# A selective scan on one core: diagonal matrices of B by way of DRAM scratch, and the next product ahead of the gate

## The chip, the core and the metric

The kernel runs on one core of one Trainium2 chip. A core has a matrix engine (PE; its weight loads are shown as PEld), a vector engine (DVE), a scalar engine (ACT), a general engine (POOL), a sync engine (SP) that here issues most of the DMAs, and 16 DMA engines. The engines run their own instruction streams and wait for each other by semaphores. The metric is the device time of one execution in microseconds, lower is better; it is the median of several runs.

## The reference

Two residual layers on x of shape 8 x 128 x 128 x 128. The first (Fourier and window attention over channels, with depthwise convolutions) is not touched by the change. The second is a Mamba block over the 16384 pixels of each image, and the change is in its scan:

```python
xz = u @ W_in
xs, z = jnp.split(xz, 2, axis=-1)
xt = conv_general_dilated(xs.T, conv_w, ...) + conv_b      # 4 taps, causal
xc = jax.nn.silu(xt)
dt, Bm, Cm = jnp.split(xc @ W_xproj, [DT_RANK, DT_RANK + D_STATE], axis=-1)
delta = jax.nn.softplus(dt @ W_dt + b_dt)
def step(hs, inp):
    d_t, B_t, C_t, u_t = inp
    dA = jnp.exp(d_t[:, :, None] * A)
    h_new = dA * hs + (d_t * u_t)[:, :, None] * B_t[:, None, :]
    y_t = jnp.einsum('bdn,bn->bd', h_new, C_t)
    return (h_new, y_t)
y = ys + xc * D_param
out = (y * silu(z)) @ W_out
```

There are 256 channels d and 16 states n, so 4096 recurrences per image, each 16384 long, in float32.

## The kernel before

The scan part cuts each image into 32 chunks of 512 pixels (`T`), 256 chunks in all. A chunk has 16 steps (`ST`). A step works on a tile of 128 partitions (4 states by 32 channels) by 512 pixels, twice (`j` = 0 and 1): so 32 scans a chunk. `where(n)` turns the running step number n into chunk, half of the channels `h` (steps 0 to 7 and 8 to 15), pair of states `mp` (0 in steps 0 to 3 and 8 to 11, else 1) and block `k`.

In step n these stand in the engines' queues:

- `product(n+1)`: on PE, 32 small matmuls that form delta*u*B for the next step in PSUM (`hb`, two buffers). The weights are `duT`, the transposed delta*u of 64 pixels; the moving operand is `bd`, 64 x 64 diagonal matrices that hold B of two states, so that a matmul multiplies each pixel by its own B. The trace counts each float32 matmul twice, so 64 per product.
- `decay(n+3)`: on ACT, two exponentials `dA`.
- `scan(n)`: on DVE, two scans `hs` over `dA` and `hb`.
- `keep_state(n-1)`: on ACT, the last column of `hs`, for the next chunk.
- `weigh(n)`: on POOL, `hc` = `hs` times C (`crep`, C repeated over partitions by DMAs).

The rest of a chunk's work is spread over the steps by a hand-written table, `beside`: a step, a chunk relative to the current one, and a function. `first` is a second table of two entries, `gate` at step 3 and `step_sizes_act` at step 7, both for the next chunk; its entries stand ahead of decay and product. Work on PE beside the products: four taps of `conv` for each half, `gate` (e_z), `xproj` (e_x), `step_sizes` (e_dt), `turn_b` (e_bt, the transposed B), `turn` (e_t), `add` (y, sums over states), `project` (e_o). On DVE beside the scans: `skip` (yt), `residual` (acc), and the diagonals. On POOL beside `weigh`: `drive` (du) and `gated` (yt).

The diagonals of B before the change: `turn_b` at step 7 transposes B on PE into PSUM, `keep_b` at step 8 copies it to `bt` with DVE. `diagonals` multiplies the constant `same` (two identity matrices of 64) with B, 1 of 8 blocks (128 x 512) at a time; DVE makes six blocks a chunk. `more_diagonals` makes the other two as 16 activations of 128 x 64 on ACT. `bd` has two buffers, one for each `mp`.

`InOrder` (lines 169 to 187) records the compute instructions of each engine so that they run in the order written; therefore nearly all instructions carry line 180 in the profile, and are told apart by their tiles. DMAs on SP are not bound by it: they stand in the order in which a scheduler put them, and SP issues them strictly one after the other. A DMA on SP also waits until the eighth DMA before it has landed.

DMAs of a chunk, all on SP: `xin` (line 1063, the input two chunks ahead, 256 KB), `cd` (line 1131, C to DRAM), `crep` (line 1140, 4 x 128 KB for `mp` 0 after `cd`, and 4 more for `mp` 1), `dld` (line 1155, delta to DRAM, 512 KB) and `dlrep` (line 1161, delta repeated over partitions, 4 x 256 KB for each half). `crep` has three buffers and `dlrep` two, so that the second half of each waits until POOL and ACT are done with an older one. Every eighth chunk a band of the image is loaded for the residual (`acc`, line 1069, 2 MB in runs of 128 bytes), and a finished band is stored by ACT's queue (2 MB, runs of 128 bytes).

Of the kernel before, what the change touches and what calls it, by code (L numbers as in the profile page):

```python
# [111 lines left out]
def _layout(a):  # L112

    a = {n: np.asarray(v) for n, v in a.items()}
    o = {"x": np.ascontiguousarray(a["x"]).reshape(B, C, HW)}
    o["consts"], o["bconsts"], o["ker"] = _constants()
    p = "L0_conv_"
    f, s = a[p + "projf_w"].reshape(C, 2 * C), a[p + "projs_w"].reshape(C, 2 * C)

    rows = np.arange(C).reshape(2, 4, 16).transpose(1, 0, 2).reshape(-1)  # L120

    j, h = np.arange(8)[:, None], np.arange(NH)[None, :]
    frows = np.concatenate([(HD * h + j).reshape(-1), (HD * h + 15 - j).reshape(-1)])
    ws = [a[p + n + "1_w"].reshape(C, C) for n in "qkv"] + [f[:, frows], f[:, C:], s[:, rows], s[:, C:]]
    o["wpack"] = np.concatenate([w.T for w in ws] + [a[p + "w1"].reshape(NK, C).T], 1)
    tf = np.repeat(a[p + "temp_f"].reshape(NH), HD)
    ts = np.repeat(a[p + "temp_s"].reshape(NH), HD)[rows]
    o["cvec"] = np.stack([a[p + n + "1_b"] for n in "qkv"] + [tf, ts], 1)
    o["bn"] = np.concatenate([a[p + n] for n in ("b1", "bn_gamma", "bn_beta", "bn_mean", "bn_var")])[None]
    w2 = np.zeros((13, NK + 1, 13, C), np.float32)  # L130
    for u in range(13):
        w2[u, :NK, u] = a[p + "w2"].reshape(C, NK).T
        w2[u, NK, u] = a[p + "b2"]

    w2 = w2.reshape(13, NK + 1, 13, C // 8, 2, 4).transpose(0, 1, 4, 3, 5, 2)
    o["w2blk"] = w2.reshape(13 * (NK + 1), 13 * C)


    taps = np.zeros((4, NG, 2, 8, 8, 2, 4, 4), np.float32)
    for n, c in enumerate("qkvc"):  # L140
        for y in range(4):
            for x in range(4):
                taps[n, :, :, y + 1 : y + 4, x + 1 : x + 4, 0, y, x] = a[p + c + "3_w"]
                taps[n, :, :, y : y + 5, x : x + 5, 1, y, x] = a[p + c + "5_w"]
    taps = taps.reshape(4, NG // 4, 4, 2, 2, 4, 2, 4, 32)
    o["taps"] = taps.transpose(2, 3, 5, 7, 1, 0, 4, 6, 8).reshape(128, -1)
    p = "L1_conv_"
    o["win"] = a[p + "W_in"]
    o["cw"] = a[p + "conv_w"].T.reshape(1, 4 * DI)

    xp = a[p + "W_xproj"].reshape(2, 128, DR + 2 * DS).transpose(1, 0, 2)
    wx = np.zeros((128, 2, 4, 32), np.float32)
    wx[:, :, :2, :DR] = xp[:, :, None, :DR]
    wx[:, :, 2, :] = xp[:, :, DR:]
    o["wx"] = wx.reshape(128, 256)
    o["wdt"] = np.zeros((128, 128), np.float32)
    for h in range(2):
        o["wdt"][32 * h : 32 * h + DR] = a[p + "W_dt"][:, h * 128 : (h + 1) * 128]
    o["same64"] = np.tile(np.eye(64, dtype=np.float32), (2, 1))
    o["gath"] = np.tile(np.eye(32, dtype=np.float32), (4, 1))  # L160
    o["wout"] = a[p + "W_out"].reshape(2, 128, C).transpose(1, 0, 2).reshape(128, -1)
    halves = [a[p + n].reshape(2, 128).T for n in ("conv_b", "b_dt", "D_param")]
    o["dvec"] = np.concatenate(halves, 1)

    o["alog"] = a[p + "A_log"].reshape(DI // 32, 32, 4, 4).transpose(2, 1, 3, 0).reshape(128, -1)
    return {n: np.ascontiguousarray(v) for n, v in o.items()}
# [24 lines left out]
def tile_kernel(ctx: ExitStack, tc: tile.TileContext, I: dict, out: bass.AP):  # L191
# [830 lines left out]
    NQ, NM, NR, NBK = 4, 4, 32, DI // 32  # L1022
    ND, NTB = 64, T // 128
    QR = 32
    with tc.tile_pool(name="e_c", bufs=1) as cp, tc.tile_pool(name="e_w", bufs=2) as wk, tc.tile_pool(
        name="e_h", bufs=4
    ) as hp, tc.tile_pool(name="e_d", bufs=3, space=DRAM) as dp, tc.tile_pool(
        name="e_b", bufs=2, space=PSUM
# [4 lines left out]
            return t  # L1033

        gath = fixed("gath", [128, NR], I["gath"])
        same = fixed("same", [128, ND], I["same64"])
        unit = fixed("unit", [128, 128], I["consts"][:, 0:128])
        win = fixed("win", [128, 2 * DI], I["win"])
        wx = fixed("wx", [128, 2, 128], I["wx"])
        wdt = fixed("wdt", [128, 128], I["wdt"])  # L1040
        wout = fixed("wout", [128, 2, C], I["wout"])
# [3 lines left out]
        nc.scalar.activation(A, A, AF.Exp)  # L1045
        nc.vector.tensor_scalar(A, A, -1.0, None, ALU.mult)

        wf = cp.tile([128, 4, DI], F32, name="wf")
        nc.sync.dma_start(wf.rearrange("p a d -> p (a d)"), I["cw"].partition_broadcast(128))
        for k in range(4):  # L1050
            nc.vector.tensor_tensor(wf[:, k, :], wf[:, k, :], win[:, 0:DI], ALU.mult)
        state = cp.tile([128, NM, NBK], F32, name="state")
        ch = {}
        total = B * NCH
        RT = T // W
# [3 lines left out]

        def load(i):  # L1060
            b, k = divmod(i, NCH)
            xin = wk.tile([128, T], F32, name="xin")
            nc.sync.dma_start(xin, X1[b, :, k * T : (k + 1) * T])
            ch[i] = {"xin": xin}

# [45 lines left out]
        def gate(i):  # L1111
            c = ch[i]
            c["sz"] = wk.tile([128, 2, T], F32, name="sz", bufs=3)
            for h in range(2):
                ps = bank("e_z", h)
                pe.matmul(ps, lhsT=win[:, DI + h * 128 : DI + (h + 1) * 128], rhs=c["u"][:, 3:], start=True, stop=True)
                act.activation(c["sz"][:, h, :], ps, AF.Silu)

        def xproj(i):
# [29 lines left out]
        def step_sizes_act(i):  # L1149
# [5 lines left out]
            nc.sync.dma_start(d.rearrange("h p t -> p h t"), c["dl"])  # L1155
            for h in range(2):
                if h:
                    repeat_c(i, 1)
                t = c["dlr", h] = wk.tile([128, 4, T], F32, name="dlrep")
                for q in range(NQ):  # L1160
                    nc.sync.dma_start(t[q * NR : (q + 1) * NR], d[h].rearrange("(k r) t -> r k t", r=NR))
# [29 lines left out]
                pe.transpose(c["bp"][:, 32 * j : 32 * j + 32], c["dbl"][rs, j * 128 : (j + 1) * 128], unit[rs, rs])  # L1191

        def keep_b(i):
            c = ch[i]
            c["bt"] = wk.tile([128, NTB, DS], F32, name="bt")
            dve.tensor_copy(c["bt"], c["bp"][:, : NTB * 32].rearrange("p (j n) -> p j n", n=32)[:, :, :DS])

        def diagonals(i, mp, j):


            c = ch[i]
            if (mp, j) in ((0, 0), (1, 0)):
                c["bd", mp] = wk.tile([128, NTB, NQ, ND, 2], F32, name="bd")
            to = [128, NQ, ND, 2]
            b = c["bp"][:, 32 * j : 32 * j + DS].rearrange("p (q m) -> p q m", m=NM)[:, :, 2 * mp : 2 * mp + 2]
            dve.tensor_tensor(
                c["bd", mp][:, j], same.unsqueeze(1).unsqueeze(3).to_broadcast(to), b.unsqueeze(2).to_broadcast(to), ALU.mult
            )

        def more_diagonals(i, which):  # L1210

            c = ch[i]
            for n in which:
                j, q, m = 2 + n // 8, n // 2 % 4, n % 2
                at = NM * q + 2 + m
                act.activation(c["bd", 1][:, j, q, :, m], same, AF.Identity, scale=c["bt"][:, j, at : at + 1])


        ST = 16
# [11 lines left out]
        def decay(n):  # L1231
            i, h, mp, k = where(n)
            for j in range(2):
                dA = hp.tile([128, T], F32, name="dA", bufs=10)
                kk = 4 * h + k
                act.activation(dA, ch[i]["dlr", h][:, k, :], AF.Exp, scale=A[:, 2 * mp + j, kk : kk + 1])
                dAs[n, j] = dA
# [69 lines left out]
        def residual(i):  # L1307
# [10 lines left out]

        beside = [
            (0, 1, lambda i: conv(i, 1, 2)),  # L1320
            (0, 0, lambda i: diagonals(i, 1, 1)),
            (0, 0, lambda i: more_diagonals(i, range(6, 11))),
            (1, 1, lambda i: conv(i, 1, 3)),
            (1, 0, lambda i: more_diagonals(i, range(11, 16))),
            (2, 1, conv_act),
            (2, -1, lambda i: add(i, 3, 0, 1)),
            (3, -1, lambda i: skip(i, 1)),
# [3 lines left out]
            (5, 0, lambda i: add(i, 0, 0)),  # L1331
            (6, 0, lambda i: add(i, 0, 1)),
            (6, 1, step_sizes),
            (7, 1, turn_b),
            (8, -1, project),
            (8, 1, lambda i: drive(i, 0)),
            (8, 1, keep_b),
            (8, 2, norm),
            (9, -1, residual),
            (9, 1, lambda i: drive(i, 1)),  # L1340
            (9, 2, lambda i: conv(i, 0, 0)),
            (10, 0, lambda i: add(i, 1, 0, 1)),
            (11, 0, lambda i: skip(i, 0)),
            (11, 1, lambda i: diagonals(i, 0, 0)),
            (11, 1, lambda i: turn(i, 0)),
            (11, 2, lambda i: conv(i, 0, 1)),
            (12, 0, lambda i: gated(i, 0)),
            (12, 1, lambda i: turn_act(i, 0)),
            (12, 1, lambda i: diagonals(i, 0, 1)),
            (12, 2, lambda i: conv(i, 0, 2)),  # L1350
            (13, 1, lambda i: diagonals(i, 0, 2)),
            (13, 1, lambda i: turn(i, 1)),
            (13, 2, lambda i: conv(i, 0, 3)),
            (14, 1, lambda i: turn_act(i, 1)),
            (14, 1, lambda i: diagonals(i, 0, 3)),
            (14, 0, lambda i: add(i, 2, 0, 1)),
            (15, 1, lambda i: diagonals(i, 1, 0)),
            (15, 1, lambda i: more_diagonals(i, range(6))),
            (15, 2, lambda i: conv(i, 1, 0, 1)),
        ]  # L1360
        first = [
# [4 lines left out]
        for n in range(-2 * ST, (total + 1) * ST):  # L1366
# [5 lines left out]
                    rows_of(i // NCH, i % NCH * RT)  # L1372
            if there((n - 1) // ST):
                keep_state(n - 1)
            for step, rel, f in first:
                if step == s and there(i + rel):
                    f(i + rel)
            if there((n + LEAD) // ST):
                decay(n + LEAD)
            if there((n + 1) // ST):  # L1380
                product(n + 1)
            if there(i):
                scan(n)
            for step, rel, f in beside:
# [23 lines left out]
```

## Time and profile before

| | |
|---|---|
| median of 3 runs | 18748.7 us (18740.43 to 18783.58) |
| profiled execution, first to last instruction | 18790.5 us |
| first scan to last | 6647 to 18763 us |
| chunk of the scan part, mean | 47.3 us |
| busy share of the whole span: PE, DVE, ACT, POOL | 88%, 76%, 64%, 70% |
| granted PE clock in the scan part | 0.99 of full speed |
| DMA engines busy in the scan part, mean | 0.45 |

The profile is of one execution. Busy time is the union of an engine's instructions; the idle time before an instruction is put down to what ended it: another engine, a DMA, or "issue" when the profile shows nothing that the engine waited for. Steps are numbered 0 to 15 within a chunk; a step is between 2.4 us (two scans) and 4.7 us long. A window's table gives busy time per engine, so that a single chunk can be set beside the mean.

### The profile page before, as it was taken

The page shows a single profiled execution, that of the slowest core. Times are in us where ns is not written, and L with a number is a line of the kernel's source. Part 1 is how long each engine was busy: PE and PEld are TensorE (multiplying, and loading weights), DVE is VectorE, ACT ScalarE, POOL GpSimd, SP SyncE. Part 2 cuts the span into 40 slices and gives each one's busy share as a digit, 9 for nine tenths or more (in the row PEclk, how much of TensorE's full clock was granted, in tenths as well). Part 3 has the DMA queues.
Part 4 walks back from the last instruction along what each step waited for, and adds up shares of the span by engine and source line. Part 5 has one row for each costly group of instructions (what it writes and reads, how often), then busy time and mean ns, then how long its engine had stood idle before and what let it go on. Part 6 is the DMA issues. An engine that isn't in the chain of part 4 may idle for free. (4 is left out here: it accounts for less than half of the span.)

```text
span 18790.5 us, 791009 instructions
## 1 busy us (share of the span) xinstructions
PE 16559.7 (88%) x353336; PEld 9548.0 (51%) x353336; DVE 14247.0 (76%) x15987; ACT 12026.1 (64%) x26077; POOL 13091.3 (70%) x7572
## 2 busy tenths in 40 slices
PE   7789988888888888999899889998999999998898
PEld 5566665555555544444444444444444444444444
DVE  6545543333444489999999999999999999999998
ACT  4443333344323377777777777777777777777777
POOL 3333334443222278899899888998898888888898
PEclk8899998889999999999999999999999999999999
DMA  9963347777777645444544454445444444444443
GB/s 377 370 220 94 93 125 226 231 236 214 201 207 208 195 98 104 97 97 97 106 97 97 97 102 97 96 97 102 97 97 97 102 101 96 95 98 101 94 97 86
DMA packets 2434567, 2601.35 MB, mean 138 GB/s; under 512 B 1221965, under 2 KB 1624013, under 8 KB 2396866
## 3 DMA queue, kind: packets, MB, share of 16 engines
q1 hardware_dynamic: 1730850, 2206.28, 44.1%
q10 hardware_dynamic: 679840, 277.32, 7.2%
q8 instruction: 2783, 45.60, 1.1%
q0 software_dynamic: 20480, 67.13, 1.1%
q14 instruction: 614, 5.03, 0.1%
HBM read 1715.23 MB, written 834.93 MB: 136 GB/s over the span
## 5 line engine op out<-in xcount | busy, mean ns | idle before, releaser
L180 POOL TENSOR_TENSOR hc<-hs,crep 128x1024 f32<-128x1024 f32 x4096 | 9646.3, 2372 | 1262.6 <-DVE hs L180 813.8
L180 DVE TENSOR_TENSOR_SCAN hs<-dA,state,hb 128x512 f32<-128x512 f32 x7936 | 9578.7, 1262 | 817.5 <-PE hb L180 744.1
L180 PEld LDWEIGHTS hb<-bd,duT 64*32 64x32 f32 x262144 | 3747.2, 106 | 3720.4 <-issue 2751.1
L180 PE MATMUL hb<-bd,duT 64*32 64x128 f32 x262144 | 4925.6, 275 | 708.2 <-issue 504.2
L180 ACT ACTIVATE dA<-dlrep,A 128x512 f32<-128x512 f32 x8192 | 5443.4, 713 | 7.9 <-ACT state L180 1.7
L180 PE MATMUL e_xc<-u,wf 128*128 128x512 f32 x4096 | 2236.0, 639 | 408.2 <-ACT u L180 361.5
L180 PE MATMUL y<-hc,gath 128*32 128x512 f32 x16384 | 2078.5, 609 | 36.8 <-issue 34.5
L180 ACT COPY state<-hs 128x2 f32<-128x2 f32 x4096 | 776.9, 190 | 1892.2 <-DVE hs L180 1874.1
L180 ACT ACT_TABLE_LOAD x1057 | 1356.1, 1283 | 338.9 <-PE e_dt L180 292.0
L180 PE MATMUL c_mm<-src,taps 32*32 32x512 f32 x32768 | 1219.9, 630 | 207.9 <-issue 175.4
L180 DVE COPY vst<-c_mm 128x512 f32<-128x512 f32 x1024 | 684.8, 689 | 741.9 <-PE c_mm L180 637.3
L180 PEld LDWEIGHTS e_xc<-u,wf 128*128 128x128 f32 x4096 | 646.5, 192 | 826.4 <-ACT u L180 430.8
L180 ACT ACTIVATE bd<-same,bt 128x64 f32<-128x64 f32 x4096 | 1054.2, 339 | 5.3 <-PE hb L180 5.1
L180 POOL TENSOR_SCALAR qm<-vst,cst 128x512 f32<-128x512 f32 x256 | 503.8, 2062 | 779.1 <-DVE vst L180 745.7
L180 PEld LDWEIGHTS c_mm<-src,taps 32*32 32x32 f32 x32768 | 680.5, 105 | 706.8 <-issue 518.3
L180 ACT ACTIVATE junk<-vst 128x256 f32<-128x256 f32 x1024 | 416.6, 410 | 942.5 <-DVE vst L180 941.3
L180 DVE TENSOR_TENSOR bd<-same,e_bt 128x512 f32<-128x512 f32 x1536 | 1019.4, 664 | 0.0
L180 PE MATMUL a_mm<-xt,wp 128*128 128x256 f32 x3072 | 763.2, 410 | 261.9 <-ACT pk L180 182.2
L180 POOL TENSOR_TENSOR eo<-eo,et 128x1008 f32<-128x1008 f32 x128 | 298.5, 2332 | 969.1 <-DVE et L180 960.6
L180 POOL DMA_DIRECT2D X<-d_x x256 | 138.4, 541 | 1072.2 <-DVE d_x L180 864.3
L180 DVE TENSOR_TENSOR d_x<-d_p,d_x 128x512 f32<-128x512 f32 x256 | 274.9, 1074 | 783.6 <-DMA d_x<-in_x 505.7
L180 PEld LDWEIGHTS a_mm<-xt,wp 128*128 128x128 f32 x3072 | 621.1, 206 | 419.5 <-ACT pk L180 195.5
(179 smaller groups left out, 19982.9 us busy)
## 6 DMA issues: line engine op xcount, KB each, us to landing
dlrep<-dld SPq DMA_DIRECT2D x2048, 256.0 KB
crep<-cd SPq DMA_DIRECT2D x2048, 128.0 KB
dld<-dl SPq DMA_DIRECT2D x256, 512.0 KB
src<-Pq SPq DMA_DIRECT2D x128, 544.5 KB
src<-Pv SPq DMA_DIRECT2D x128, 544.5 KB
src<-Pk SPq DMA_DIRECT2D x128, 544.5 KB
src<-Px SPq DMA_DIRECT2D x128, 544.5 KB
xt<-in_x SPq DMA_DIRECT2D x64, 1024.0 KB
```

Source lines behind the costliest of these rows:

```text
L180: made = method(*args, **kwargs)
```

## The change

It has these parts.

- `diagonals`, `more_diagonals` and `same` go. Four DRAM scratch tensors `diag` (128 rows of 2048 floats, 1 MB each; two per `mp`, used by alternate chunks) are filled with zeros once. `keep_b`, now an ACT copy, writes B of each chunk onto their diagonals by four DMAs of 64 x 16 runs of two floats. `load_b` loads a whole matrix back, 1 MB, as `bd`, which has three buffers now. `load_b` for `mp` 0 stands inside `step_sizes_act` behind the loads of `dlrep` for the first half, for `mp` 1 at step 8.
- `turn_b` goes from step 7 to 5, `keep_b` from 8 to 6, and `norm` (the input of the chunk after next, on ACT) from 8 to 6.
- In each step `product(n+1)` stands ahead of the table `first` and of decay. On PE that changes step 3 alone, where `gate` is in `first`.
- To make room: `win` keeps only the half that `gate` reads (the other is used once, for `wf`), `xin` has one buffer instead of two, `dA` nine instead of ten.

In the scheduled program SP's order for a chunk becomes: `cd`, `xin`, one write of `diag`, four `crep`, three writes of `diag`, `dld`, `load_b` for `mp` 0, four `dlrep`, four `crep`, four `dlrep`, `load_b` for `mp` 1. `load_b` for `mp` 0 waits for both writes to its tensor.

```diff
+    cp = ctx.enter_context(tc.tile_pool(name="e_c", bufs=1))
+    wf = cp.tile([128, 4, DI], F32, name="wf")
+    nc.sync.dma_start(wf.rearrange("p a d -> p (a d)"), I["cw"].partition_broadcast(128))
+    DROW = NTB * NQ * ND * 2
+    diag = {(n, mp): dram.tile([128, DROW], F32, name=f"diag{n}{mp}") for n in range(2) for mp in range(2)}
+    with tc.tile_pool(name="e_0", bufs=1) as zp:
+        win_x = zp.tile([128, DI], F32, name="win_x")
+        nc.sync.dma_start(win_x, I["win"][:, 0:DI])
+        for k in range(4):
+            nc.vector.tensor_tensor(wf[:, k, :], wf[:, k, :], win_x, ALU.mult)
+        zero = zp.tile([128, DROW], F32, name="zero")
+        nc.gpsimd.memset(zero, 0.0)
+        for d in diag.values():
+            nc.sync.dma_start(d, zero)
...
-            xin = wk.tile([128, T], F32, name="xin")
+            xin = wk.tile([128, T], F32, name="xin", bufs=1)
...
             for h in range(2):
                 if h:
+                    load_b(i, 0)
                     repeat_c(i, 1)
...
         def keep_b(i):
             c = ch[i]
-            c["bt"] = wk.tile([128, NTB, DS], F32, name="bt")
-            dve.tensor_copy(c["bt"], c["bp"][:, : NTB * 32].rearrange("p (j n) -> p j n", n=32)[:, :, :DS])
-
-        def diagonals(i, mp, j):
...
-        def more_diagonals(i, which):
...
+            bt = wk.tile([128, NTB, DS], F32, name="bt")
+            act.copy(bt, c.pop("bp")[:, : NTB * 32].rearrange("p (j n) -> p j n", n=32)[:, :, :DS])
+            for mp in range(2):
+                d = diag[i % 2, mp]
+                for x in range(2):
+                    ap = [[DROW + 2, ND], [2 * ND, NTB * NQ], [1, 2]]
+                    to = bass.AP(d.tensor, d.offset + x * ND * DROW, ap)
+                    frm = bt[ND * x : ND * x + ND].rearrange("p j (q m) -> p (j q) m", m=NM)[:, :, 2 * mp : 2 * mp + 2]
+                    nc.sync.dma_start(to, frm)
+
+        def load_b(i, mp):
+            t = ch[i]["bd", mp] = wk.tile([128, NTB, NQ, ND, 2], F32, name="bd", bufs=3)
+            nc.sync.dma_start(t.rearrange("p j q t m -> p (j q t m)"), diag[i % 2, mp])
...
-                dA = hp.tile([128, T], F32, name="dA", bufs=10)
+                dA = hp.tile([128, T], F32, name="dA", bufs=9)
...
-            (7, 1, turn_b),
+            (6, 2, norm),
+            (5, 1, turn_b),
             (8, -1, project),
             (8, 1, lambda i: drive(i, 0)),
-            (8, 1, keep_b),
-            (8, 2, norm),
+            (6, 1, keep_b),
+            (8, 1, lambda i: load_b(i, 1)),
...
             if there((n - 1) // ST):
                 keep_state(n - 1)
+            if there((n + 1) // ST):
+                product(n + 1)
             for step, rel, f in first:
                 if step == s and there(i + rel):
                     f(i + rel)
             if there((n + LEAD) // ST):
                 decay(n + LEAD)
-            if there((n + 1) // ST):
-                product(n + 1)
```

The removed entries of `beside` are the nine of `diagonals` and `more_diagonals`.

## The prediction

> **What bounds the kernel now.** I read first the page's totals, then a table of windows over the scan part and over single chunks, the groups of the scan part, the timeline of one step, and last the waits.
>
> The windows (length, then busy us of PE, PEld, DVE, ACT, POOL, clock, DMA share, GB/s): the whole scan part, then an ordinary chunk, then the two chunks in which a finished band of the image is stored and a new one loaded.
>
> ```profile
> 6646.00:18763.00 12117.00, 10933.85 (x289696) 5674.28 (x289681) 11237.39 (x10744) 9521.18 (x20196) 10868.54 (x5124) 0.99 0.45 97
> ...
> 11377.60:11423.00 45.40, 42.44 (x1142) 21.96 (x1148) 43.75 (x43) 37.16 (x80) 42.41 (x21) 1.00 0.34 89
> 11565.70:11613.50 47.80, 42.63 (x1133) 22.03 (x1133) 44.06 (x42) 37.50 (x82) 42.83 (x21) 1.00 0.55 103
> 11613.50:11667.40 53.90, 45.68 (x1133) 23.20 (x1133) 44.28 (x43) 36.74 (x77) 41.72 (x21) 0.94 0.85 140
> ```
>
> The scan part is 12117 of 18790.5 us: 256 chunks of 47.33 us. In the ordinary chunk DVE is busy 43.75 of 45.4 us, but PE and POOL stand at 42.4, only 1.3 us behind: taking work from DVE alone pays until these two bind. The same work costs 8.5 us more where the DMA share is 0.85.
>
> The groups of the scan part (count | busy, mean ns | idle before it and who ended that):
>
> ```profile
> L180 POOL TENSOR_TENSOR hc<-hs,crep 128x1024 f32<-128x1024 f32 x4096 | 9646.3, 2372 | 1262.6 <-DVE hs L180 813.8 <-PE e_x L180 189.6 <-POOL yt L180 56.5
> L180 DVE TENSOR_TENSOR_SCAN hs<-dA,state,hb 128x512 f32<-128x512 f32 x7936 | 9578.7, 1262 | 817.5 <-PE hb L180 744.1 <-ACT dA L180 31.9 <-POOL hc L180 18.1
> ...
> L180 ACT ACTIVATE bd<-same,bt 128x64 f32<-128x64 f32 x4096 | 1054.2, 339 | 5.3 <-PE hb L180 5.1
> L180 DVE TENSOR_TENSOR bd<-same,e_bt 128x512 f32<-128x512 f32 x1531 | 1016.4, 664 | 0.0
> ```
>
> DVE's second loss is its wait for hb, here where step 3 of the ordinary chunk puts the gate ahead of the product on PE (PE, then DVE):
>
> ```profile
> 11386.49 1.99 PE L180 MATMUL e_z<-u,win 128*128 128x512 f32 x4 [0.22 <-ACT xc L180]
> 11388.41 2.03 PE L180 MATMUL hb<-bd,duT 64*32 64x128 f32 x128
> ```
>
> ```profile
> 11389.72 2.45 DVE L180 TENSOR_TENSOR_SCAN hs<-dA,state,hb 128x512 f32<-128x512 f32 x2 [1.42 <-PE hb L180]
> ```
>
> The waits of PE over 6800 to 18700 us (251.4 chunks), in total us and times, and one gap in the slow chunk:
>
> ```profile
> PE hb L180 <- issue: 500.0, 471, 4.0
> PE e_xc L180 <- ACT u L180: 353.5, 241, 1.7
> PE hb L180 <- DVE hs L180: 163.4, 440, 2.4
> ```
>
> ```profile
> 11634.68 1.76 PE L180 MATMUL hb<-bd,duT 64*32 64x128 f32 x50 [3.39 <-issue]
> ```
>
> An "issue" gap in the middle of one product's matmuls waits for no data. The page has 2783 instruction packets of 16 KB; 256 instructions of 64 bytes each would be 712,448, and PE and PEld together ran 706,672. So I read these gaps as PE's code arriving late. All issue waits of PE (500.0 on hb, 34.3 on y, 16.1 on e_xc, 2.7 on e_t) are 553 us, 2.2 us a chunk. They go with DMA: in the three chunk windows the DMA engines worked 15.4, 26.3 and 45.8 us (share times length), and by the means over all chunks at these two places of the band (48.7 and 52.35 us, share 0.577 and 0.85, against 46.3 at 0.36) each added us of DMA work cost 0.22 us of time.
>
> **The change, part by part, in us per chunk.**
>
> 1. *Diagonals leave DVE and ACT.* DVE loses 6 x 0.664 (rows above; 3.5 to 4.0 after overlap at the ends) and the bt copy of 0.198. ACT loses 16 x 0.339 and gains the copy of bt, 0.2 by DVE's row; ACT is busy 37.2 and idle the rest, so this is worth nothing by itself.
>
> 2. *product(n+1) ahead of gate.* Decay is on ACT and step_sizes_act has no matmul, so on PE only step 3 changes: 1.42 us of DVE idle go. e_z then follows the product, and sz and the next table load on ACT are about 1.2 us later; the decays run three steps ahead, some 7 us, so nothing waits.
>
> 3. *norm from step 8 to step 6.* conv(0) at step 9 finds u ready: PE's 353.5/251.4 = 1.4 us go. It is hidden under DVE today, and counts once PE binds. ACT's steps 6 and 7 take 1.2 us more; e_o behind dl waits perhaps 0.4, within the rounding.
>
> What is then left: DVE 45.4 - 3.6 - 1.4 = 40.3; POOL 42.4; PE 42.4 busy plus its other waits in the ordinary chunk (0.4 on hs, 0.2 on xc, and 0.3 I allow for the acc of step 9, which holds DVE and so the next product): **43.3**, PE-bound, between 42.4 (no wait at all) and 44.5. Before, the same count without issue gaps gives 47.35 - 2.2 = 45.1.
>
> 4. *New DMA traffic.* keep_b writes 4 x 1024 runs of 8 bytes, 256 per DMA engine. No packet of 8 bytes is in the trace of this part; its 4-byte packets took 12.7 ns, the 128-byte ones of the band's store to DRAM 16.9 and of its load 22.6. Nearest in kind is the store: 4.3 us (3.2 to 5.8). load_b adds 2 x 1 MB in rows of 8 KB; such packets took 326 ns in the first part, 16 per engine: 5.2 us (up to 8.7 at the 136 ns of the 2 KB packets). Together 9.5 (8.4 to 14.5) on top of 0.45 x 47.35 = 21.3: a share of 0.66.
>
> 5. *What this costs PE's code.* The 1.46 us of issue gaps in ordinary chunks stand against 16.8 us of DMA work: 0.087 each, if all is put down to it. The band's traffic costs 0.22, in bursts of some 17 us. Loads at 0.087: 0.45. The small writes resemble the band, but in a burst of 4 us that one fetch can outlast: midway, 0.15 x 4.3 = 0.65. Sum **1.1**, between 0 (8-byte writes leave the queue free for the code) and 14.5 x 0.22 = 3.2. Nothing hides it where PE binds.
>
> 6. *Waits on SP.* The bt copy comes some two steps earlier, near 11397 in the ordinary chunk's time; the writes land by about 11404, where by SP's timeline it issues dlrep anyway (11403.75) after waiting for dld. Behind load_b(0), which waits for the writes, stand dlrep for h = 0, crep, dlrep for h = 1 and load_b(1). dlrep(0) lands about 7 us after issue and is due at step 13, 11414, and three steps of decay ahead cover 7 more. load_b(1) is due at step 3 of the next chunk, some six steps or 17 us after its turn on SP. In the two band chunks of eight I allow 0.8 each, **0.2** on average (0 to 0.5). xin with one buffer is loaded after norm and has ten steps. dA with 9 buffers still holds four steps of two.
>
> 7. *Once:* 4 MB of zeros (128 rows of 8 KB each, 2.6 us per MB) before the first chunk, while SP's constants took from 6593 to 6610 already: about 5 us.
>
> Sum: 43.3 + 2.2 + 1.1 + 0.2 = 46.8 against 47.35, so -0.55 x 256 + 5, about -135 us. The profiled execution is 18790.5 us, 0.2% over the median of 18748.7; taken from the median: **18,615**.
>
> The Trainium skill speaks against part 4 in "DMA: Bandwidth & Descriptors", section Rules for kernel authors: transfers under 64 KB are mostly overhead, and each write here is 8 KB. The nearest row, the 16 KB cd write, made SP wait 406.2/303 = 1.3 us. At that page's two microseconds of fixed cost each, four in a row would be 8 us, still before dlrep is due.
> Its "Runtime: NRT & Kernel Launch", section Instruction fetch mechanics, calls the crossing of a 16 KB block mostly hidden; the 500 us row differs. By the page the 1.1 falls away, and the time would be about 18,330.
>
> **Rivals.**
>
> *The code fetch does not suffer* (the gaps are the band's alone): 43.3 + 2.2 + 0.2 = 45.7, -1.65 x 256, about 18,330. For it: no 8-byte burst lasts 17 us. Against: ordinary chunks have gaps too.
>
> *PE's code becomes the bound* (slower). Place: issue gaps inside hb. Small runs at 22.6 ns and loads at 8.7 us, 14.5 us at 0.15 to 0.22, cost 2.2 to 3.2: with 0.4 of lateness 48.1 to 49.1 a chunk, 18,940 to 19,200. It decides from 1.6 us more of gaps on. For it: 53.9 us at share 0.85. Against: that burst is four times longer.
>
> *The diagonals come late.* If 8-byte runs took over some 50 ns (no row shows it), the writes outlast the 6 us before dlrep and then its cover, and product(0) waits at step 15 for bd: each further us is one per chunk, 19,300 and more.
>
> *It comes out even:* 1.6 of gaps, the gain given back: 18,750.
>
> **How the numbers follow.** My forecast 0.34 (own range 18,450 to 18,710), no suffering 0.13, even 0.12, code bound 0.32, late diagonals 0.09. Faster 0.47, within 0.2% (37 us, about what three runs can tell) 0.12, slower 0.41. The range 18,300 to 19,150 leaves out the better half of the second case and the dear ends of the last two.
>
> **What would show it.** DVE busy near 40 and PE's near 42.5 per chunk; the 1.42 us before step 4 gone and no wait of e_xc for u: parts 1 to 3. PE's issue waits a chunk: near 3.3 for me, near 2.2 for the first rival, over 3.8 for the second. SP waiting long for the diagonal writes, or PE for bd, would be the third. I am wrong if PE waits for DVE or POOL instead, or if chunks away from the bands pass 47 us.

## The result, and the profile after

The changed kernel takes 19672.0 us (median of 4 runs, 19656.4 to 19696.5) against 18757.7 beside it: ratio 1.0492, 95% interval 1.0478 to 1.0506. It is slower by some 914 us; the forecast was 18,615, and 19,150 was the end of its range. The profiled execution has a span of 19671.4 us.

The table of windows of the changed kernel (length, then busy us of PE, PEld, DVE, ACT, POOL, clock, DMA share, GB/s): the whole scan part, an ordinary chunk, and the two chunks in which a band is stored and loaded.

```profile
6624.00:19645.00 13021.00, 11199.96 (x289664) 5788.05 (x289663) 10427.99 (x8958) 8489.52 (x16353) 10854.28 (x5123) 0.96 0.63 132
12933.60:12982.70 49.10, 43.16 (x1133) 22.38 (x1134) 40.75 (x35) 33.85 (x66) 42.03 (x21) 0.97 0.57 131
13946.60:13996.40 49.80, 43.97 (x1133) 22.52 (x1133) 41.12 (x36) 33.98 (x67) 43.54 (x21) 0.97 0.66 132
13996.40:14056.30 59.90, 46.73 (x1133) 23.76 (x1133) 40.91 (x36) 33.93 (x66) 41.60 (x21) 0.91 1.06 174
```

A chunk takes 50.9 us instead of 47.3. DVE's work fell as forecast, from 43.75 to 40.75 in the ordinary chunk, yet that chunk went from 45.4 to 49.1. No engine is full: PE, the fullest, is busy 43.16 of 49.1. Its clock is 0.96 where it was 0.99.

The groups of the scan part (count | busy, mean ns | idle before it and who ended that):

```profile
L179 DVE TENSOR_TENSOR_SCAN hs<-dA,state,hb 128x512 f32<-128x512 f32 x7936 | 9596.3, 1266 | 2488.0 <-PE hb L179 2211.5 <-POOL hc L179 100.3 <-ACT dA L179 98.2
L179 ACT ACTIVATE dA<-dlrep,A 128x512 f32<-128x512 f32 x8186 | 5434.0, 713 | 1270.8 <-DMA dlrep<-dld 1264.7
```

DVE's wait for hb rose from 744.1 to 2211.5 us: PE sets the pace. ACT waits 1264.7 us for a DMA that it did not wait for before. PE's own waits, 6800 to 19500 us (249.5 chunks; total us, times, longest):

```profile
PE hb L179 <- issue: 816.5, 554, 5.9
PE e_bt L179 <- ACT dbl L179: 326.9, 242, 1.4
PE hb L179 <- DMA bd<-diag: 195.1, 31, 7.4
PE e_o L179 <- ACT dl L179: 168.9, 242, 0.7
```

The wait of e_xc for u is gone. In its place stand e_bt's wait for dbl, a wait for bd, and more issue.

Two steps of the ordinary chunk in the timeline: first step 3 (part 2 of the prediction), then step 5, where turn_b now stands:

```profile
12944.07 1.16 PE L179 MATMUL hb<-bd,duT 64*32 64x128 f32 x64
12945.15 1.99 PE L179 MATMUL e_z<-u,win 128*128 128x512 f32 x4
12945.78 2.44 DVE L179 TENSOR_TENSOR_SCAN hs<-dA,state,hb 128x512 f32<-128x512 f32 x2
...
12953.58 0.43 PE L179 MATMUL e_bt<-unit,dbl 32*128 32x32 f32 x4 [1.36 <-ACT dbl L179]
12953.94 1.16 PE L179 MATMUL hb<-bd,duT 64*32 64x128 f32 x64
12955.25 2.45 DVE L179 TENSOR_TENSOR_SCAN hs<-dA,state,hb 128x512 f32<-128x512 f32 x2 [1.42 <-PE hb L179]
```

In step 3 the product now stands ahead of e_z and the scan waits for nothing: the 1.42 us are gone. In step 5 the same 1.42 us are back. turn_b, moved there from step 7, needs dbl, which ACT copies in that very step; PE waits 1.36 us with the next product queued behind e_bt, and DVE waits for that product.

PE's balance per chunk, from the waits and busy times between 7000 and 18000 us (busy and waits add up to the chunk), with the experiments told of below:

| us per chunk | chunk | PE busy | clock | issue | dbl | bd | duT | dl | hs | u |
|---|---|---|---|---|---|---|---|---|---|---|
| before | 47.35 | 42.73 | 0.99 | 2.23 | 0 | 0 | 0 | 0 | 0.65 | 1.41 |
| changed | 50.90 | 43.81 | 0.96 | 3.60 | 1.31 | 0.79 | 0.45 | 0.67 | 0.21 | 0 |
| e1, no added traffic | 46.21 | 42.16 | 0.99 | 1.74 | 1.26 | 0 | 0 | 0.69 | 0.34 | 0 |
| e2, e1 with turn_b at 7 | 44.80 | 42.34 | 0.99 | 1.79 | 0 | 0 | 0.01 | 0.41 | 0.14 | 0 |
| e3, loads only | 48.43 | 42.95 | 0.98 | 3.06 | 1.24 | 0.16 | 0 | 0.65 | 0.35 | 0 |
| e4, writes only | 48.03 | 42.95 | 0.98 | 2.50 | 1.22 | 0 | 0.48 | 0.67 | 0.19 | 0 |
| e5, before with two moves | 46.19 | 42.62 | 0.98 | 1.74 | 0 | 0 | 0 | 0.42 | 1.36 | 0 |
| e9, writes by ACT | 51.51 | 44.04 | 0.95 | 2.68 | 1.25 | 0.32 | 0.01 | 3.15 | 0.01 | 0 |
| e10, e9 with an order held | 49.89 | 43.90 | 0.96 | 3.32 | 0 | 0.91 | 0.01 | 0.41 | 1.22 | 0 |
| e12, loads in quiet steps | 46.42 | 43.04 | 0.98 | 2.68 | 0 | 0.13 | 0 | 0.25 | 0.22 | 0 |
| e13, loads in busy steps | 52.33 | 44.63 | 0.93 | 5.67 | 0 | 0 | 1.28 | 0.46 | 0.11 | 0 |

(Columns from issue on are what PE waited for. Smaller waits are left out.)

The DMA rows of one ordinary chunk, in 40 slices of 1.1 to 1.2 us from its first scan on (busy tenths), of the kernel before and of the changed one:

```profile
DMA  0000000000000000101629516699100039857999
```

```profile
DMA  9850000000000000012838944999899999999999
```

Nearly all of a chunk's transfers start from dbl and dl, near its middle. Before, the second half had gaps; now it is full to the end and three slices into the next chunk, and the third of the chunk behind these still stands idle.

### The profile page after: what moved, and what is told of

Read it like the earlier page. It is cut to its first block, busy times and chain, and to the rows that moved or that the text cites. A ratio compares the mean times of both kernels' runs of the same rounds, so it can differ in the third digit from the quotient of the medians.

```text
span 19671.4 us, 788131 instructions
## 1 busy us (share of the span) xinstructions
PE 16808.1 (85%) x353336; PEld 9653.8 (49%) x353336; DVE 13443.6 (68%) x14195; ACT 10994.9 (56%) x22237; POOL 13085.9 (67%) x7573
## 3 DMA queue, kind: packets, MB, share of 16 engines
q8 instruction: 2783, 45.60, 1.0%
## 4 chain that ended last, share of the span: by engine, by line
PE 54%; ACT 15%; DMA 14%; issue 9%; DVE 5%; SPq 1%; POOL 1%; ACTq 0%; DVEq 0%; POOLq 0%
PE hb L179 14%; PE e_xc L179 8%; ACT dA L179 6%; PE c_mm L179 6%; PE y L179 5%; ACT L179 4%; DMA dlrep<-dld 3%; PE e_z L179 3%; DVE hs L179 2%; PE a_mm L179 2%; DMA d_of<-OFL 2%; DMA dld<-dl 2%; PE d_b L179 2%; PE c_gram L179 2%; PE d_p L179 2%
## 5 line engine op out<-in xcount | busy, mean ns | idle before, releaser
L179 DVE TENSOR_TENSOR_SCAN hs<-dA,state,hb 128x512 f32<-128x512 f32 x7936 | 9596.3, 1266 | 2488.0 <-PE hb L179 2211.5
L179 ACT ACTIVATE dA<-dlrep,A 128x512 f32<-128x512 f32 x8192 | 5437.8, 713 | 1270.8 <-DMA dlrep<-dld 1264.7
L179 PE MATMUL hb<-bd,duT 64*32 64x128 f32 x262144 | 5057.8, 280 | 1246.1 <-issue 837.4
L179 PEld LDWEIGHTS hb<-bd,duT 64*32 64x32 f32 x262144 | 3803.5, 108 | 4347.2 <-issue 3333.9
L179 PE MATMUL e_xc<-u,wf 128*128 128x512 f32 x4096 | 2357.0, 670 | 44.0 <-issue 24.8
L179 PE MATMUL y<-hc,gath 128*32 128x512 f32 x16384 | 2106.5, 608 | 49.0 <-issue 47.3
L179 ACT ACTIVATE sz<-e_z 128x512 f32<-128x512 f32 x512 | 305.4, 597 | 940.5 <-PE e_z L179 940.5
L179 PEld LDWEIGHTS y<-hc,gath 128*32 128x32 f32 x16384 | 417.9, 109 | 815.6 <-issue 785.7
```

What stands on the lines that cost most here:

```text
L179: made = method(*args, **kwargs)
```

## The experiments

Three theories were written down ahead. (In e1 to e4, e12 and e13 the added traffic, or the writes of B, are left out and `bd` holds zeros: these runs give a price, not a kernel to use.) A: three separate losses (PE's code late under DMA load, dlrep late on SP, e_bt waiting for dbl). B: the added traffic alone. C: the engine part of the forecast (parts 1 to 3) was wrong.

**e1 and e2: the added traffic away, then turn_b back.**

```diff
+        still = cp.tile([128, NTB, NQ, ND, 2], F32, name="still")
+        nc.sync.dma_start(still.rearrange("p j q t m -> p (j q t m)"), diag[0, 0])
...
-                    nc.sync.dma_start(to, frm)
...
-            t = ch[i]["bd", mp] = wk.tile([128, NTB, NQ, ND, 2], F32, name="bd", bufs=3)
-            nc.sync.dma_start(t.rearrange("p j q t m -> p (j q t m)"), diag[i % 2, mp])
+            ch[i]["bd", mp] = still
```

e2 in addition:

```diff
-            (5, 1, turn_b),
+            (7, 1, turn_b),
...
-            (6, 1, keep_b),
+            (8, 1, keep_b),
```

> The changed kernel without its new DMAs: no writes of the diagonals and no load per chunk; bd is one constant tile that holds zeros, so the scan's driving term is left out. Everything else stays. Theory A (three separate losses: PE's code comes late under the DMA load, dlrep lands late, and PE waits for dbl at e_bt since turn_b stands in step 5): the first two go, the third stays: issue gaps back to about 2.2 us a chunk, ACT no longer waits for dlrep, e_bt's wait of 1.3 us stays; 43.3 + 2.2 + 1.3 = 46.8 us a chunk, about 18,600 us. Theory B (all of the loss is the traffic): 43.3 + 2.2 = 45.5 us a chunk, about 18,300 us. Theory C (the engines' coupling was misjudged and 43.3 is out of reach): 48 us or more a chunk, 18,900 us and up.

> As e1_no_traffic, with turn_b back at step 7 and keep_b at step 8. Theory A: e_bt no longer waits for dbl, 1.3 us a chunk less than e1_no_traffic, about 330 us, near 18,300 us. Theory B: the same time as e1_no_traffic within 40 us, since that wait is hidden.

Measured: e1 18497.3 us, 0.9851 (0.9811 to 0.9891); e2 18170.2 us, 0.9677 (0.9638 to 0.9716). So the added traffic costs 19672 - 18497 = 1175 us, and the place of turn_b 327 us (theory A expected 330), measured without the traffic; the two together are more than the whole loss. No run moves turn_b back alone in the changed kernel, where PE waits 1.31 us a chunk for dbl as against 1.26 in e1. Theory C falls: without both, a chunk takes 44.80 us, of which 1.79 are issue, so 43.0 stand against the 43.3 of the prediction.

**e3 and e4: each half of the traffic alone** (the changed kernel without the writes, and with the writes but a constant bd).

> The changed kernel with its loads of bd, but without the writes of the diagonals (the scratch stays zero, so the scan's driving term is left out). Theory A: the loads share the queue with dld and dlrep and stand ahead of dlrep: half of the late dlrep stays (ACT waits 2 to 3 us a chunk for it) and issue gaps are near 3.2 us; about 48.3 us a chunk, 19,000 us. If the small writes do the harm: close to e1_no_traffic, within 100 us.

> The changed kernel with its writes of the diagonals, but without the loads (bd is one constant tile of zeros, so the scan's driving term is left out). Theory A: the four writes hold SP some 3 us longer ahead of dld, and add little DMA time (256 x 8.5 ns = 2.2 us): issue gaps near 2.6 us, dlrep 3 us late of which the three steps of decay hide most; about 47.3 us a chunk, 18,750 us. If the small writes do the harm: 49 us or more a chunk, 19,200 us and up.

Measured: e3 19070.8 us, 1.0157 (1.0117 to 1.0197); e4 18959.2 us, 1.0093 (1.006 to 1.0126). Over e1 the loads cost 573 us, the writes 462, and 140 more come when both are there. The balance shows different paths. The loads raise issue by 1.32 us a chunk. The writes raise it by 0.76 and make ACT wait for dlrep (1001 us in all, 4.4 a chunk), behind which the second copy of duT comes late for the product (0.48). Both raise PE's busy time by 0.8 at a lower clock. In e3 the scheduler put both loads of bd behind dlrep, for which ACT then hardly waits (4.6 us in all), so e3 doesn't show what a load ahead of it costs. e4 lies between the two cases of its expectation.

**e5 and e6: the other parts alone**, in the kernel before. e6 puts the product ahead of the first table, e5 also moves norm to step 6.

```diff
+            (6, 2, norm),
...
-            (8, 2, norm),
...
+            if there((n + 1) // ST):
+                product(n + 1)
             for step, rel, f in first:
```

> The kernel before with two of the change's moves alone: product ahead of the first table, and norm at step 6 instead of 8. No diagonals by DRAM, turn_b stays at step 7. Theory A: DVE's 1.42 us ahead of step 4 go, DVE is left with 43.8 us of work; with the issue gaps of 2.2 that PE can now partly hide behind it, 45.9 us a chunk, about 18,400 us. If the moves were worth nothing without lighter DVE: 18,700 us or more.

> The kernel before with the product ahead of the first table and nothing else. Theory A: PE's wait of 1.7 us for u at step 9 stays, but DVE is busy with acc there, so it is hidden: within 60 us of e5_before_product_norm. Rival: PE is close enough to binding that the wait counts: 150 us or more over e5_before_product_norm.

Measured: e5 18448.5 us, 0.984 (0.9822 to 0.9858); e6 18566.0 us, 0.99 (0.9885 to 0.9915). e5 is faster than both kernels. Its step 3 went from 4.73 to 3.21 us on average. In e6 PE still waits 1.62 us a chunk for u, and the 118 us between the two fall between what was expected for it.

**e7 and e8: SP's order.** Theory A took the late dlrep for a matter of order, which the timeline of the changed kernel seemed to show (SP, then ACT):

```profile
12959.27 3.77 SPq L1216 DMA_DIRECT2D diag<-bt  x3
...
12963.13 0.61 SPq L1165 DMA_DIRECT2D dld<-dl  x1
...
12964.48 0.34 SPq L1220 DMA_DIRECT2D bd<-diag  x1
...
12967.83 1.75 SPq L1172 DMA_DIRECT2D dlrep<-dld  x4
...
12977.16 1.33 ACT L179 ACTIVATE dA<-dlrep,A 128x512 f32<-128x512 f32 x2 [4.97 <-DMA dlrep<-dld]
```

ACT had dl ready at 12959.8, but SP was issuing writes until 12963.0; the decay that needs dlrep starts 9.3 us after its issue. e7 holds the load of bd behind dlrep; e8 moves turn_b to step 7 and holds SP to dld, the four writes, dlrep, bd.

```diff
-                    nc.sync.dma_start(t[q * NR : (q + 1) * NR], d[h].rearrange("(k r) t -> r k t", r=NR))
+                    (sp if h == 0 else nc.sync).dma_start(t[q * NR : (q + 1) * NR], d[h].rearrange("(k r) t -> r k t", r=NR))
...
-            nc.sync.dma_start(t.rearrange("p j q t m -> p (j q t m)"), diag[i % 2, mp])
+            (nc.sync if mp else sp).dma_start(t.rearrange("p j q t m -> p (j q t m)"), diag[i % 2, mp])
```

(e7; `sp` is `InOrder(tc, nc.sync)`. In e8 dld, the writes, dlrep, bd and the second crep are all issued through `sp`.)

> The changed kernel with one order on SP held: the load of bd for mp 0 behind the four dlrep of the first half, instead of ahead of them. Theory A (dlrep is late by the writes that hold SP and by this load on the same rings): dlrep lands 1 to 2 us earlier, ACT's wait for it falls from 4.9 us a chunk to about 3, about 1 us a chunk gained, 19,400 us. If the loads' harm is on PE's code alone: 19,650 us. If bd is then late itself: PE waits for bd, 19,700 us or more.

> The changed kernel with turn_b and keep_b at step 7, and SP's order held as dld, four writes of the diagonals, dlrep of the first half, bd for mp 0, crep, dlrep of the second half, bd for mp 1: the writes no longer stand ahead of dld. The traffic is the same. Theory A: e_bt's wait of 1.3 us goes and ACT's wait for dlrep falls to under 1 us; the issue gaps of 4.5 us stay; 44.8 (e2_no_traffic_turn7) + 2.5 = 47.3 to 48 us a chunk, 18,800 to 18,950 us. Theory B (the traffic itself does it, through PE's code): 19,300 us.

Measured: e7 19837.3 us, 1.0578 (1.0561 to 1.0595); e8 19769.9 us, 1.0542 (1.0525 to 1.0559). Both are slower than the changed kernel. e7 came out as the third case of its expectation: ACT waits less for dlrep (3.6 a chunk for 5.0), and PE more for bd (1.43 for 0.79). e8 missed both of its cases: dlrep goes out 4.6 us earlier in the chunk (median) and turn_b's wait is gone, yet ACT still waits 4.8 us a chunk for dlrep, and PE's issue rises to 4.80 and its busy time to 44.74. So e8 changed the order and didn't bring dlrep in time.

**e9 and e10: the writes on ACT's queue**, so that SP has nothing between dl and dlrep but dld.

```diff
-                    nc.sync.dma_start(to, frm)
+                    act.dma_start(to, frm)
```

(e9: the changed kernel. e10: e8, where keep_b stands behind dl.)

> The changed kernel, but keep_b issues its four writes of B on ACT's queue, right behind its copy of bt, instead of on SP's. Nothing is left out. In the changed kernel SP issues dld 3.3 us after ACT is done with dl (26.7 and 29.96 us from the chunk's start), dlrep for the first half 5.3 us after dld (3.6 before the change), and ACT waits 4.9 us a chunk for it. Theory A (the writes stand in SP's queue ahead of dld): dld follows dl within half a us. ACT is held 2.7 to 5 us by issuing ahead of dl (the mean issue on SP was 0.65 us, the fourth up to 2.1), which eats most of it: dl is late by what SP gains. Then about 19,450 to 19,650 us, a little under the changed kernel's 19,672. Theory B (it is all traffic: 8-byte runs and loads hold the DMA engines, whoever issues them): within 30 us of 19,672. If ACT's issuing costs more than SP's, over 19,750.

> As e8 (turn_b back at step 7, SP's order held: dld, dlrep for the first half, the load of mp 0, crep, dlrep for the second half, the load of mp 1), but the four writes are issued by ACT behind dl and the first decay of step 7. Nothing is left out. SP then has nothing between dl and dlrep but dld, as in the kernel before (where dlrep went out 3.6 us after dld). e8 took 19,770 with dlrep still late. Theory A (place in SP's queue, and the turn of e_bt): dlrep goes out near 27 to 28 us from the chunk's start (26.9 before the change, 30.6 in e8), ACT's wait for it falls from 4.9 us a chunk to under 2, PE's wait for dbl is gone; the loads alone with the turn at step 7 would be 19,071 - 327 = 18,744, and the writes' share of issue gaps 0.5 us a chunk makes 18,870: so 18,800 to 19,100. Theory B (the traffic itself): no better than 19,350, which is the changed kernel less the 327 us of the turn.

Measured: e9 19818.6 us, 1.0564 (1.0546 to 1.0582); e10 19377.5 us, 1.0322 (1.0293 to 1.0352). In e9 ACT issues for 3.8 us ahead of dl, and PE waits 3.15 us a chunk for dl. That is more than SP won: the third case that its expectation names. e10 brings dlrep in time, as PE's and ACT's waits between 7000 and 18000 us show:

```profile
PE hb L179 <- issue: 653.9, 423, 5.2
PE hb L179 <- DVE hs L179: 267.9, 269, 3.4
...
ACT dA L179 <- DMA dlrep<-dld: 79.9, 56, 3.3
```

With dlrep in time e10 is still at theory B's end: 295 us under the changed kernel, about what turn_b's place is worth, and 1207 over e2, as the traffic cost 1175 in the changed kernel. So theory A's 18,800 to 19,100 is not reached. But e10 has a price of its own: with the writes on ACT, step 10 takes 3.79 us on average for 2.38, and PE waits 1.22 us a chunk for hs, for 0.21. Whether the late dlrep cost something that this hides isn't settled; no run has dlrep in time without such a price.

**e11: one more diagonal block on ACT**, in e5 (24 activations, five DVE blocks).

> e5 (the kernel before with the product ahead of the first table and norm at step 6, 18,448.5 us), with one more of the eight diagonal blocks made by ACT: 24 activations of 128x64 a chunk instead of 16, and five DVE blocks instead of six. Nothing is left out. If DVE still bounds e5 (busy 43.8 of 46.2 us a chunk), 0.664 us a chunk go: 18,280 to 18,330. If PE bounds it as much as DVE (the floor of 43 to 43.3 us that the prediction had for PE), under 60 us: 18,390 to 18,450. ACT goes from some 37.3 to 40 us busy; if its longer steps 15 to 2 hold up PE's products, slower than 18,450.

Measured: 18495.8 us, 0.9861 (0.9843 to 0.9878). DVE's work fell by 0.5 us a chunk and the time did not: DVE no longer bounds e5 alone.

**What an issue gap is.** The records settle this without a further run. The matmuls, weight loads and semaphore events of PE, numbered in order of time, make 712,451 records in the changed kernel, and 2783 instruction packets of 16 KB (256 times 64 bytes) would hold 712,448. All 458 issue gaps over 0.5 us between 7000 and 18500 us, 782 us in all, end at a record whose number is 193 modulo 256 (the first matmul, or the weight load just ahead of it). The timeline of the ordinary chunk (PE's matmuls alone) lets it be counted:

```profile
12975.43 0.43 PE L179 MATMUL hb<-bd,duT 64*32 64x128 f32 x9 [2.13 <-issue]
12975.79 0.66 PE L179 MATMUL e_t<-unit,du 128*128 128x128 f32 x4
12976.28 1.02 PE L179 MATMUL e_xc<-u,wf 128*128 128x512 f32 x2
12977.24 1.16 PE L179 MATMUL hb<-bd,duT 64*32 64x128 f32 x64
12978.33 1.92 PE L179 MATMUL y<-hc,gath 128*32 128x512 f32 x16
12980.18 0.67 PE L179 MATMUL hb<-bd,duT 64*32 64x128 f32 x32
12981.86 0.67 PE L179 MATMUL hb<-bd,duT 64*32 64x128 f32 x32 [1.01 <-issue]
```

From one gap to the next there are 9 + 4 + 2 + 64 + 16 + 32 = 127 matmuls, as many weight loads, and two semaphore events: 256. Both gaps cut a product in the middle.

There is one code packet per block of 256. It takes 1.1 to 1.2 us on average in every run, loaded or not; what varies is when it starts. Packets and blocks are taken one for one in order, so that the packet which starts around a block's begin brings the next block; by this no block begins before its packet has ended, and 99 of 100 begin 1.2 us after that or later. When the packet starts 2 to 3 us after the block's begin, a quarter to a third of the next blocks come late (by over 0.3 us); at 3 to 4 us, most of them (blocks between 7000 and 18000 us, mean gap in us):

```
packet starts after   kernel before          changed kernel
                      blocks  late  mean gap   blocks  late  mean gap
under 1 us              546    1%    0.01        598    0%    0.00
1 to 2                  815    5%    0.03        526    5%    0.04
2 to 3                  369   25%    0.21        320   29%    0.26
3 to 4                  165   70%    0.76        205   60%    0.67
over 4                  172   91%    1.65        274   88%    1.95
```

The share of blocks whose packet starts after 3 us or more is 16% before and 25% in the changed kernel. The gaps at these block ends add up to 2.24 and 3.59 us a chunk, as PE's issue waits do (2.23 and 3.60).

What holds the packet up shows in the same records. In the changed kernel 806 of these blocks begin with the DMA engines under half busy in the first 2 us (by the packets that start there, code left out): 2 of their packets start after 3 us or more. 763 begin with the engines over 90% busy: there it is 441, and of the 777 us of gaps 709 stand behind these blocks. Before the change 458 blocks began with engines so busy, 222 of them with a packet that late.

**e12 and e13: the same loads in a quiet and in a busy stretch.** This was what stood open: does the amount of traffic delay the code, or its packing? Both are e2 with the two loads, issued by ACT in halves of 64 partitions.

```diff
+            t, r = ch[i]["bd", mp], slice(64 * g, 64 * g + 64)
+            act.dma_start(t[r].rearrange("p j q t m -> p (j q t m)"), diag[i % 2, mp][r])
...
+            (0, 0, lambda i: load_b(i, 1, 0)),
+            (1, 0, lambda i: load_b(i, 1, 1)),
+            (3, 1, lambda i: load_b(i, 0, 0)),
+            (4, 1, lambda i: load_b(i, 0, 1)),
```

(e12; in e13 the steps are 10 and 11 for `mp` 0 and 12 and 13 for `mp` 1.)

> As e2 (no writes of B, so the scratch stays zero; turn_b at step 7, keep_b at 8; 18,170 us with a constant bd), with the two loads of a whole matrix back, 1 MB each as in the changed kernel, but issued by ACT in halves of 64 partitions at steps 0 and 1 (mp 1 of the running chunk) and 3 and 4 (mp 0 of the next), where in the traces of this study the DMA engines stand nearly idle. The twin, e13, issues the same halves in steps 10 to 13. In the trace one code packet of PE belongs to a block of 256 instructions and the next block begins no sooner than some 1.3 us after that packet's end, so a packet that waits in a queue for over 2.4 us stops PE. Theory of packing (a code packet waits behind what is queued at that moment): in a quiet stretch four half loads of some 1.5 us each hardly reach 2.4 us: issue gaps 1.8 to 2.3 us a chunk (e2 has 1.77), 18,200 to 18,400 us. Theory of volume (each us of DMA work costs the same wherever it lies): gaps as in e3, some 3.2 us a chunk, and 19,071 - 327 = 18,744, give or take 80.

> The twin of e12: the same four half loads by ACT, at steps 10 and 11 (mp 0 of the next chunk) and 12 and 13 (mp 1), among the loads of crep and dlrep. The writes of B are left out as there. Both theories: issue gaps 3 to 3.7 us a chunk and 18,650 to 18,850 us. If it is near e12, the place of a load does not matter, and the difference between e2 and e3 is volume.

Measured: e12 18534.1 us, 0.9885 (0.9868 to 0.9901); e13 19993.0 us, 1.0661 (1.0645 to 1.0677). The same bytes from the same engine differ by 1459 us. DMA rows of an ordinary chunk of e12 and of e13:

```profile
DMA  9817910000003899602071999005999501699998
```

```profile
DMA  9100000000000001289834978999999999989930
```

PE's issue waits between 7000 and 18000 us, e12 and then e13:

```profile
PE hb L179 <- issue: 560.2, 485, 5.1
```

```profile
PE hb L179 <- issue: 1109.6, 439, 6.1
```

Place weighs more than volume: issue is 2.68 us a chunk in e12 and 5.67 in e13, against 1.79 without the loads, and the share of packets that start after 3 us or more is 17% and 29% against 13%. Not all of the 1459 us is code: in e13 ACT also waits 3.1 us a chunk for dlrep (0.3 in e12), and PE 1.28 for duT. Both sizes were missed. e12 is 364 us above e2 and above what packing was to cost (18,200 to 18,400), so the loads aren't free there either, and e13 is far above the 18,744 that e3 led to: from ACT's queue, beside SP's, the busy stretch was worse than behind SP's own loads. Whether that is the second queue or the step wasn't tried apart. In the whole computation half of e12's place could not be had: the matrix for `mp` 0 is due at step 15, before the next quiet stretch.

## Why the prediction was wrong

The step that failed is the price of the new transfers (parts 4 to 6): 1.1 + 0.2 = 1.3 us a chunk were put down for them, and they cost 4.7 (50.90 less 46.21 in e1), of which 1.86 is issue, 1.65 longer busy time of PE, for which there was no term, and 1.24 PE's waits for bd and duT (other waits fell by 0.1). Beside it, the move of turn_b was counted at nothing and cost 1.4 (e1 less e2).

- *Parts 1 to 3 held.* DVE is busy 40.75 us in the ordinary chunk (about 40 forecast). The 1.42 us before step 4 and e_xc's wait for u are gone. The floor of 43.3 us was 43.0 in e2.
- *The move of turn_b was left out.* The prediction counted the writes that come earlier with it, but not what e_bt itself waits for in step 5. dbl is copied there. It is 1.31 us a chunk in PE's waits, and 327 us by e1 less e2 (set against a loss of 914), readable from the diff and the table of steps alone.
- *Part 4 held as an amount.* 8-byte packets took 8.5 ns (16.9 taken), so 2.2 us of DMA time for 4.3; the 8 KB packets took 405 ns (326 taken), so 6.5 for 5.2. The DMA share became 0.63 (0.66 forecast). But the writes lie over 7.1 us, from the first packet to the last, while little else moves, and push all later loads together.
- *Part 5 named the right place and undersized it:* issue is 3.60 us where 3.3 were forecast, but that is partly luck. Without the traffic issue is 1.74 (e1), not the 2.2 carried over, so the traffic added 1.86 where 1.1 was put. Nor did its rule hold: no single price per us of DMA work fits, as e12 and e13 gave 0.9 and 3.9 us for the same bytes.
- *Part 6 was mis-sized:* 0.2 us was allowed for lateness on SP; PE waits 0.79 for bd and 0.45 for duT, 1.24 in all. The chain in which ACT stands 4.9 us a chunk in front of dlrep was seen, but the cover of three steps was taken as enough; SP issued dld 3.2 us behind dl and dlrep 5.4 behind dld, against almost nothing and 3.0 before (medians).
- *PE's clock was left out.* The prediction showed 45.68 us of PE work at a clock of 0.94 in the band chunk and made no term of it. PE's busy time was carried over as 42.4 and became 43.81. Without the traffic it is 42.16 at 0.99, and over the runs it rises, but for small differences, as the clock falls (44.63 at 0.93 in e13). It is 1.4 us a chunk, and no step of the prediction had it; the last section works it out.
- *The sum:* 1.31 + 1.4 + 1.04 (1.24 for 0.2) + 0.3 = 4.05 us a chunk over the forecast of 46.8; measured 4.1. The 0.9 us that the floor held for other waits came out (0.67 on dl, 0.21 on hs).
- *The rivals.* "The diagonals come late" asked for 50 ns per 8-byte run: 8.5, so not for that reason, though PE did wait for bd. "PE's code becomes the bound" is nearest: its 18,940 to 19,200 and turn_b's 327 make 19,270 to 19,530. Its measure was over 3.8 of issue; 3.60 was seen, with 1.4 of clock that it didn't know of. "The code fetch does not suffer" is out.
- *Part 7:* the first scan starts at 6624 us (6647 before): the zeros cost nothing that can be seen.

The page "Runtime: NRT & Kernel Launch" of the Trainium skill (Instruction fetch mechanics), which calls the crossing of a 16 KB block mostly hidden, describes 80% of the crossings of the kernel before and 75% of the changed one by these records (no gap over 0.3 us); the rest are the issue waits.

## What to carry to other kernels

Where PE runs hundreds of thousands of small matmuls, as here, its code is a stream of DMA of its own, one packet per 256 instructions, and by the table of this case the packet must start within some 2 to 3 us of a block's begin. So look at the DMA row slice by slice, not at its mean: the same 2 MB a chunk cost 364 us more than e2 where the row shows zeros (e12) and 1823 where it shows nines (e13). And for every entry that a diff moves, ask what its first instruction waits for in its new step, before counting what it feeds: here the two moves of e5 were worth 316 us by themselves, and the third, turn_b, cost 327.

## What the runs showed of the hardware

PE's clock drops after its gaps. The window table of the changed kernel in a band chunk, 4 us each:

```profile
14006.00:14010.00 4.00, 1.17 (x12) 0.13 (x4) 2.76 (x3) 0.02 (x1) 4.00 (x2) 1.00 1.09 229
14010.00:14014.00 4.00, 0.22 (x9) 0.25 (x17) 0.00 (x0) 0.00 (x0) 1.86 (x2) 0.70 1.10 310
14014.00:14018.00 4.00, 4.00 (x67) 2.46 (x53) 2.06 (x2) 0.16 (x1) 0.00 (x0) 0.50 1.65 145
```

PE was busy 1.4 of 8 us; then it works a whole 4 us at half clock. So it is throughout: between 7000 and 18000 us there are 194 stretches of half clock (72 before the change, 57 in e1), every one of them begins after 4 us in which PE was busy for at most 65%, and each lasts 3.4 us or a multiple of it. At half clock the matmuls of a product follow each other every 24.4 ns instead of 14.3.

The page "TensorE: Matmul & The Clock Gate" of the Trainium skill (Part 1: The HAM clock gate) describes such a half rate after an idle window of some 3.4 us, released by as long a time of activity. The length agrees; but PE needn't have been idle throughout, as it was busy for 40% (median) of the 4 us ahead.

So a long stall is paid for twice. Between e1 and the changed kernel PE's busy time rose by 1.65 us a chunk, nearly as much as its issue waits (1.86). An estimate from the figures above puts 1.2 of the 1.65 down to half clock: PE was busy at half clock for 0.84 us a chunk in e1 and 3.47 in the changed kernel, and something over 0.4 of such time is lost. With that share taken off, PE's busy time is 41.8 to 42.3 us in all fifteen kernels; what makes the rest differ wasn't looked into.

The packets of 8 bytes took 8.5 ns each by the records, half of what the 128-byte ones had led to, and still the four writes, 32 KB a chunk, cost 462 us by themselves (e4 less e1), against 573 for 2 MB of loads (e3 less e1).
